# Attention and scan on one core: sums and products of the side work taken later, softmax sums inverted on chip

## The chip, the cores and the metric

The kernel runs on one core of one Trainium2 chip. The metric is device time in microseconds (us). Three timed runs of the kernel before gave 12563.84, 12565.47 and 12583.97 us; the median is 12565.47 us. Its profiled execution took 12592.85 us.

## The reference

Sixteen images of 256 channels by 1024 positions go through two layers, each added to its input after a group norm of 16 groups.

Layer 0 is attention with four heads of 32 and a small feed-forward part:

```
tok = group_norm(x) + pos
q, k, v = layer_norm(tok) @ w_qkv
out = softmax(q k' / sqrt(32)) v
tok = out @ w_out + b_out + tok
tok = gelu(layer_norm(tok) @ w_ff1 + b_ff1) @ w_ff2 + b_ff2 + tok
x = x + tok
```

Layer 1 is a selective scan of 512 channels with 64 states over the 1024 positions. With delta, B, C and u computed from the group-normed x (projection, causal convolution of four taps, silu, softplus):

```
h[t] = exp(delta[t] * A) * h[t-1] + delta[t] * u[t] * B[t]      (512 x 64 states)
y[t] = sum over states of h[t] * C[t]
x = x + ((y + u * D) * silu(z)) @ w_o * sigmoid(conv(x))
```

All is float32 at the interface.

## The kernel before

**The scan sets the beat.** For each image the 512 x 64 states are cut into 256 units of 128 rows by 1024 positions; 16 images make 4096 units. One unit takes, in the order in which the loop records it: a load of `dub` (delta times u, repeated over the states) six units ahead on SP's queue; `inputs`, a GpSimd multiply of `dub` with `bt` four units ahead (L977); a part of `outputs`, in which TensorE multiplies finished states `h` with C into `yb` (L1019, L1031) and ScalarE copies `y` and `yo` out; `scan` on VectorE (L994); and `decay` two units ahead, two TensorE products (L986) and one exponential on ScalarE (L988) into the PSUM tile `a`. There are two buffers of `a`, so the products for unit n+2 wait until scan n has read its own.

**Side work.** Everything else of the next image (`prepare`: `first_norm`, `attention_layer`, `scan_inputs`) and the end of the image before (`gate_and_store`) is written as generators. Each `yield w` ends a step; `w` is its share. After `scan` and `decay` of a unit the loop takes the next steps that are due:

```
return share if share < 1 else max(1.0, share / rate)
```

`rate` is chosen so that all shares of an image fill 247 units. A step's instructions thus stand on each engine's queue behind that unit's scan (VectorE), decay products (TensorE) and exponential (ScalarE). At the end of the kernel each of PE, ACT, DVE and POOL is bound to the order in which instructions were recorded. The first image's `prepare` runs alone, before any scan; I call that the prologue. The preparation of the other 15 images runs beside the scan of the image before.

**Places that the change touches.** In `group_norm` TensorE sums squares or values over channels into `gn_m_ps` or `gn_v_ps` (L275), `mean_of` reduces that on VectorE (L282), ScalarE makes the mean (L293) or the inverse root (L309, L310), and VectorE subtracts (L297) or multiplies (L313). It runs twice per image. In `attention_layer` the keys come out of TensorE as `qk_ps` (L431), ScalarE copies them to `k4` (L435), VectorE takes the difference `kd` of the two halves (L448), and the row maxima follow (L473, L481, L453). Then for two pairs of heads and two halves of the queries eight steps each make scores `st_ps` (L547), their exponentials `pt` (L555) and the products with the values, `av` (L535); the last product of a half is followed in the same step by `evacuate`, which copies 32 rows of the output to `ao` (L523) and 32 rows of the softmax sums to `sums` (L524), and the second head of the pair follows a step later. The sums go to DRAM (`den`), come back as a 128 x 32 tile `few`, are inverted (L579), go to DRAM again and come back repeated over 32 rows each; VectorE multiplies `ao` with them (L591). `o_ps` (L600) and `f_ps` (L618, L635) are the output and feed-forward products, added to the tokens at L596, L605 and L631. L615 adds the tokens to x. In `scan_inputs` `project` (L706, L711, L712) makes u, and `tap` (L720) is its convolution.

PSUM: beside the scan the side work has two banks of the pool `mm` through `psum`, and with `psum3` also the bank that holds `av`.

Of the kernel before, what the change touches and what calls it, by code (L numbers as in the profile page):

```python
# [19 lines left out]
P = 128  # L20
# [30 lines left out]
def attention_then_scan_kernel(  # L51
# [63 lines left out]
    def psum(name, dims=P):  # L115
        return (bank(mm, name) if beside["scan"] else free_bank(name))[:dims]
# [7 lines left out]
    def work(name, n=L):  # L124
        return wide.tile([P, L + 2 + CONV], F32, name=name, tag="wide")[:, :n]
# [4 lines left out]
    def hs(h):  # L130
        return ts(h, HL)
# [140 lines left out]
    def group_norm(src, dst):  # L272
        def sum_of(part, sums, k):
            for h in range(2):
                nc.tensor.matmul(  # L275
                    sums, share, part[:, hs(h)],
                    start=(k == 0 and h == 0), stop=(k == KC - 1 and h == 1),
                )

        def mean_of(sums):  # L280
            m = small.tile([P, NG], F32, name="gn_s", tag="gn_s")
            nc.vector.tensor_reduce(  # L282
                m, sums.rearrange("p (h g t) -> p g h t", g=NG, t=2), AX.XY, ALU.add
            )
            return m

        s = psum("gn_m_ps")
        sum_of(src[0], s, 0)
        yield 1
        sum_of(src[1], s, 1)  # L290
        yield 1
        m = s[:, :NG]
        nc.scalar.copy(m, mean_of(s))  # L293
        yield 1
        qs = []
        for k in range(KC):
            nc.vector.tensor_tensor(grouped(dst[k]), grouped(src[k]), over_group(m), ALU.subtract)  # L297
            q = work("gn_sq")
            nc.scalar.activation(q, dst[k], AF.Square)
            qs.append(q)  # L300
            yield 1
        s = psum("gn_v_ps")
        sum_of(qs[0], s, 0)
        yield 1
        sum_of(qs[1], s, 1)
        del qs, q
        yield 1
        v = s[:, :NG]
# [56 lines left out]
    def fetches(to, src, n=KC):  # L365
        return [partial(fetch, to, src, k) for k in range(n)]
# [18 lines left out]
    def attention_layer(b):  # L385
# [41 lines left out]
        for i in range(2):  # L427
            for hf in range(2):
                ps = psum("qk_ps")
                for k in range(KC):  # L430
                    nc.tensor.matmul(  # L431
                        ps, wqk_s[:, k, ts(i, P)], xn[k][:, hs(hf)], start=(k == 0), stop=(k == KC - 1)
                    )
                if i == 1:
                    nc.scalar.copy(k4[:, hs(hf)], ps)  # L435
                else:
                    for e in range(2):
                        nc.scalar.activation(
                            qm[hf][:, :, ts(e, 64)], ps.rearrange("p (c q) -> p c q", q=64),
                            AF.Identity, scale=even[:, e : e + 1],  # L440
                        )
                yield 1.5
# [2 lines left out]

        mx = small.tile([P, 2 * 2 * NJ], F32, name="mx", tag="mx")
        kd = hwork("kd")
        nc.vector.tensor_tensor(kd, k4[:, hs(0)], k4[:, hs(1)], ALU.subtract)  # L448
        waiting = []

        def maxima():
# [69 lines left out]
        def evacuate(pair, hf, e):  # L521
            h, o = 2 * pair + e, 2 * DH * e
            nc.scalar.copy(ao[ts(h, DH), hs(hf)], av[o : o + DH])  # L523
            nc.scalar.copy(sums[ts(h, DH), hs(hf)], av[o + DH : o + 2 * DH])  # L524

        for pair in range(HEADS // 2):
            qa, ka = qas[pair], kas[pair]
# [36 lines left out]
            yield 1  # L564


        den = dram.tile([2, HEADS, L], F32, name="den", tag="den")
        nc.sync.dma_start(den[0], sums[::DH, :])
        few = small.tile([P, HEADS * L // P], F32, name="few", tag="few")
        rows = [den[i].rearrange("h (p c) -> (h p) c", c=HEADS * L // P) for i in range(2)]  # L570
        yield 1
        nc.sync.dma_start(few, rows[0])
        yield 1
        tok = []
        for go in fetches(tok, kept):
            go()
            yield 0.5
        yield 0.5
        nc.vector.reciprocal(few, few)  # L579
        yield 1  # L580
        nc.sync.dma_start(rows[1], few)
        yield 1
        for h in range(HEADS):
            nc.sync.dma_start(sums[ts(h, DH)], den[1, h : h + 1].partition_broadcast(DH))
            if h % 2 == 1:
                yield 0.5
        yield 0.5
        yield 0.5
        outs = []
        for hf in range(2):  # L590
            nc.vector.tensor_tensor(ao[:, hs(hf)], ao[:, hs(hf)], sums[:, hs(hf)], ALU.mult)  # L591
            for k in range(KC):
                for i, ps in outs:
                    if i == k:
                        t = tok[k][:, hs(0)]
                        nc.vector.scalar_tensor_tensor(t, ps, col("b_out", k), t, ALU.add, ALU.add)  # L596
            outs.clear()
            for k in range(KC):
                ps = psum("o_ps")
                nc.tensor.matmul(ps, wout_s[:, 0, ts(k, P)], ao[:, hs(hf)], start=True, stop=True)  # L600
                outs.append((k, ps))
            yield 1.3
        for k, ps in outs:
            t = tok[k][:, hs(1)]
            nc.vector.scalar_tensor_tensor(t, ps, col("b_out", k), t, ALU.add, ALU.add)  # L605
        del outs, ps
        yield 1.2

        xs = []
        xn = [work("xn2") for _ in range(KC)]  # L610
# [1 line left out]
        hdn = work("hdn")  # L612
        f1 = []
        for hf in range(2):
            nc.vector.tensor_tensor(xs[hf], xs[hf], tok[hf], ALU.add)  # L615
            ps = psum("f1_ps")
            for k in range(KC):
                nc.tensor.matmul(  # L618
                    ps, wff1_s[:, k, :], xn[k][:, hs(hf)], start=(k == 0), stop=(k == KC - 1)
                )  # L620
            f1.append(ps)
            yield 1.1
# [1 line left out]
            table("gelu")  # L624
            nc.scalar.activation(hdn[:, hs(hf)], f1[hf], AF.Gelu, bias=col("b_ff1"))
        yield 2
        outs = []
        for hf in range(3):
            for k, ps in enumerate(outs):
                t = xs[k][:, hs(hf - 1)]  # L630
                nc.vector.scalar_tensor_tensor(t, ps, col("b_ff2", k), t, ALU.add, ALU.add)  # L631
            outs = []
            for k in range(KC if hf < 2 else 0):
                ps = psum("f2_ps")
                nc.tensor.matmul(ps, wff2_s[:, 0, ts(k, P)], hdn[:, hs(hf)], start=True, stop=True)  # L635
                outs.append(ps)
            yield 1.2
        state[b]["xs"] = xs
        state[b]["xr"] = dram.tile([C, L], F32, name="xr", tag="xr")

    def scan_inputs(b):
# [104 lines left out]
        project(0, 0)  # L746
        yield 1
        project(0, 1)
        yield 1
        for d in range(ND):  # L750
            for t in range(2):
                tap(d, t)
# [438 lines left out]
```

## Time and profile before

| | |
|---|---|
| timed runs, median | 12565.47 us |
| profiled execution | 12592.85 us, span 12590.8 us, granted TensorE clock 0.820 |
| DVE busy | 11064.3 us (88%) |
| POOL busy | 10050.9 us (80%) |
| PE busy | 9574.8 us (76%) |
| ACT busy | 7506.0 us (60%) |
| DMA share of the hardware queue | 65.3% |
| one scan (L994), mean | 2273 ns, 4096 of them |
| one `dub` multiply (L977), mean | 2404 ns, 4096 of them |
| first `few` inversion, in the prologue | at 234.51 us |

In the answers of the trace a line reads: start, length, engine, source line, operation, out<-in, shape, count, and in brackets how long the engine was idle before and what ended that. In the list of waits the numbers are total us, how often, and the longest. In the table of stretches each engine has its busy time and, in brackets, its number of instructions, then the granted TensorE clock, the share of DMA time and GB/s. TensorE's float32 products appear as two records each, so `x4` is two instructions.

### The profile page before, as it was taken

The page shows a single profiled execution, that of the slowest core. Times are in us where ns is not written, and L with a number is a line of the kernel's source. Part 1 is how long each engine was busy: PE and PEld are TensorE (multiplying, and loading weights), DVE is VectorE, ACT ScalarE, POOL GpSimd, SP SyncE. Part 2 cuts the span into 40 slices and gives each one's busy share as a digit, 9 for nine tenths or more (in the row PEclk, how much of TensorE's full clock was granted, in tenths as well). Part 3 has the DMA queues.
Part 4 walks back from the last instruction along what each step waited for, and adds up shares of the span by engine and source line. Part 5 has one row for each costly group of instructions (what it writes and reads, how often), then busy time and mean ns, then how long its engine had stood idle before and what let it go on. Part 6 is the DMA issues. An engine that isn't in the chain of part 4 may idle for free.

```text
span 12590.8 us, 419601 instructions
## 1 busy us (share of the span) xinstructions
PE 9574.8 (76%) x183984; PEld 5140.4 (41%) x183984; DVE 11064.3 (88%) x7355; ACT 7506.0 (60%) x10792; POOL 10050.9 (80%) x4233
## 2 busy tenths in 40 slices
PE   6686877868778687886868778687786877868777
PEld 2343434434344343443434344343443434434344
DVE  2788998989989899898989989899898998989998
ACT  3565665656656565665656656566565655656554
POOL 0587878878788787887878878787887878878798
PEclk8887988879788797987879888797887978879756
DMA  1566666676766766666676666766666666676666
GB/s 53 189 229 238 224 221 234 228 243 215 232 235 226 240 225 228 232 226 234 227 238 219 225 233 225 243 218 226 231 227 236 219 225 236 224 239 225 229 238 225
DMA packets 1070400, 2819.80 MB, mean 224 GB/s; under 512 B 324433, under 2 KB 402513, under 8 KB 1068562
## 3 DMA queue, kind: packets, MB, share of 16 engines
q1 hardware_dynamic: 1068562, 2792.97, 65.3%
q8 instruction: 1437, 23.54, 0.8%
q14 instruction: 401, 3.28, 0.1%
HBM read 2513.82 MB, written 261.62 MB: 220 GB/s over the span
## 4 chain that ended last, share of the span: by engine, by line
DVE 37%; PE 31%; issue 13%; ACT 8%; DMA 7%; POOL 3%; SPq 1%; DVEq 0%; POOLq 0%; ACTq 0%
DVE h L994 28%; PE a L986 5%; PE yb L1019 5%; ACT a L988 4%; DMA dub<-dus 3%; POOL dub L977 3%; PE av L535 2%; DVE over L453 2%; PE st_ps L547 2%; PE m_ps L908 2%; PE z_ps L684 2%; PE s_ps L473 2%; DMA xs<-ud 2%; DVE u L720 1%; PE gn_v_ps L275 1%
## 5 line engine op out<-in xcount | busy, mean ns | idle before, releaser
L977 POOL TENSOR_TENSOR dub<-dub,bt 128x1024 f32<-128x1024 f32 x4096 | 9752.7, 2404 | 2130.0 <-DMA dub<-dus 1928.2
L994 DVE TENSOR_TENSOR_SCAN h<-a,dub 128x1024 f32<-128x1024 f32 x4096 | 9166.7, 2273 | 596.0 <-ACT a L988 314.3
L988 ACT ACTIVATE a<-a,acol 128x1024 f32<-128x1024 f32 x4096 | 4466.1, 1090 | 3125.6 <-PE a L986 3065.8
L986 PE MATMUL a<-pieces,pick 48*128 48x512 bf16 x8192 | 1875.8, 448 | 2444.5 <-DVE h L994 2333.4
L1019 PEld LDWEIGHTS yb<-h,cd 128*32 128x32 f32 x131072 | 2433.3, 126 | 2822.9 <-issue 1601.6
L1019 PE MATMUL yb<-h,cd 128*32 128x64 f32 x131072 | 3189.4, 248 | 341.0 <-ACT y L1025 203.3
L986 PEld LDWEIGHTS <-pick 48*128 48x128 bf16 x8192 | 594.4, 95 | 2852.7 <-issue 2194.0
L1025 ACT COPY y<-yb 128x256 f32<-128x256 f32 x2048 | 766.5, 374 | 699.1 <-PE yb L1019 691.4
L1031 PE MATMUL yb<-turn,y 128*32 128x16 f32 x32768 | 590.7, 214 | 5.3 <-issue 4.4
L555 ACT ACTIVATE pt<-st_ps 128x512 f32<-128x512 f32 x1024 | 554.3, 599 | 63.8 <-PE st_ps L547 62.6
L535 PE MATMUL av<-pt,vv 128*64 128x512 f32 x2048 | 588.9, 655 | 3.8 <-ACT sums L524 1.6
L547 PE MATMUL st_ps<-sp 33*128 33x512 f32 x2048 | 573.6, 626 | 3.3 <-ACT pt L555 3.3
L1031 PEld LDWEIGHTS yb<-turn,y 128*32 128x32 f32 x32768 | 572.4, 159 | 6.0 <-issue 4.5
L1035 ACT COPY yo<-yb 128x128 f32<-128x128 f32 x512 | 136.4, 266 | 488.9 <-PE yb L1031 472.3
L734 PE MATMUL g_ps<-xp,w 128*128 128x512 f32 x732 | 406.9, 668 | 0.0
L473 PE MATMUL s_ps<-kd,qm 64*128 64x512 f32 x1022 | 340.6, 612 | 21.2 <-DVE kd L448 14.6
L453 DVE CUSTOM_DVE_ANT_0 over<-s_ps,over 128x512 f32<-128x512 f32 x512 | 325.9, 671 | 24.7 <-PE s_ps L473 24.4
L720 DVE SCALAR_TENSOR_TENSOR u<-up,cwh,u 128x1024 f32<-128x1024 f32 x192 | 295.8, 1541 | 28.0 <-ACT u L712 27.7
L481 ACT ACTIVATE over<-s_ps 128x512 f32<-128x512 f32 x511 | 275.2, 594 | 41.4 <-PE s_ps L473 41.4
L908 PE MATMUL m_ps<-xs,w 128*128 128x512 f32 x504 | 279.2, 704 | 10.2 <-POOL xs L887 9.4
L706 PE MATMUL u_ps<-xp,w 128*128 128x512 f32 x512 | 280.0, 674 | 1.5 <-ACT u L712 1.4
L661 POOL TENSOR_TENSOR xp<-xp,xs 128x1024 f32<-128x1024 f32 x32 | 75.1, 2349 | 254.1 <-DVE xp L313 246.5
(183 smaller groups left out, 7316.7 us busy)
## 6 DMA issues: line engine op xcount, KB each, us to landing
dub<-dus SPq DMA_DIRECT2D x4096, 512.0 KB
dps<-pc SPq DMA_DIRECT2D x384, 128.0 KB
pieces<-dps SPq DMA_DIRECT2D x1024, 48.0 KB
xs<-in_x_dram SPq DMA_DIRECT2D x64, 512.0 KB
xs<-kept SPq DMA_DIRECT2D x64, 512.0 KB
zs<-z SPq DMA_DIRECT2D x64, 512.0 KB
ud<-u SPq DMA_DIRECT2D x64, 512.0 KB
dus<-du SPq DMA_DIRECT2D x64, 512.0 KB
```

The source lines that it names most:

```text
L453: nc.vector.tensor_tensor_reduce(r, s, r, 1.0, -3.0e38, ALU.add, ALU.max, mx[:, at : at + 1])
L473: nc.tensor.matmul(s, qm[c // NJ][r, c % NJ], keys[r], start=True, stop=True)
L535: nc.tensor.matmul(av[ts(e, 2 * DH)], vv[j // (NJ // 2)][:, j % (NJ // 2), 2 * pair + e, :], pts[e], start=(j == 0), stop=(j == NJ - 1),)
L547: nc.tensor.matmul(s, ka[r, ts(j, P)], qa[r, hs(hf)], start=True, stop=True)
L555: nc.scalar.activation(pt, s, AF.Exp)
L977: nc.gpsimd.tensor_tensor(v, v, blocks[units[n][0]]["bt"], ALU.mult)
L986: nc.tensor.matmul(a[:, hs(hf)], w, pieces[r], start=True, stop=True)
L988: nc.scalar.activation(a, a, AF.Exp, scale=acol[:, at : at + 1])
L994: nc.vector.tensor_tensor_scan(now["h", e][:, i, :], decays.pop(n), loaded.pop(n), 0.0, ALU.mult, ALU.add)
L1019: nc.tensor.matmul(yb[ts(g, 32), ts(s, 64)], cd[:, at // 16, ts(c, 32)], hbuf[:, :, at : at + 8], start=(c == 0), stop=(c == 1),)
L1025: nc.scalar.copy(y2[:, r], yb[:, :256])
L1031: nc.tensor.matmul(some[ts(r, 32), x], y2[:, r, x:256:8], turn[:, x], start=True, stop=True)
```

## The change

- `group_norm`: the step after the last sum product has share 2 instead of 1, for the mean and for the variance.
- `kd` is taken from `k4`'s first half and the second half's PSUM tile; a step of share 1 follows it.
- `evacuate` copies the sums on VectorE instead of ScalarE.
- The four DMAs through `den` (seven issues per image) go. Eight TensorE products with columns of the identity turn the sums into a 128 x 32 PSUM tile `few_ps`; VectorE inverts it; ScalarE repeats it over 32 columns per head (`wide_few`, 128 x 1024); eight products with the identity turn that back into two PSUM tiles `inv_ps`, which VectorE multiplies into `ao`.
- Output and feed-forward products go through `outputs_of`: two products, then one at a time, each added a step after it was made; their PSUM tiles use the third bank too.
- The addition of the tokens to x (before L615) moves from VectorE to GpSimd.
- In `scan_inputs` the step behind `project(0, 1)` has share 2 instead of 1.

The sum of an image's shares goes from 272.3 to 279.2 (254.9 to 261.8 without the gate of an earlier image), so `rate` goes from 1.183 to 1.235 and steps with shares above 1.2 come a little closer together.

```diff
@@ group_norm
         sum_of(src[1], s, 1)
-        yield 1
+        yield 2
         m = s[:, :NG]
 ...
         sum_of(qs[1], s, 1)
         del qs, q
-        yield 1
+        yield 2
@@ attention_layer
                     nc.scalar.copy(k4[:, hs(hf)], ps)
+                    keys = ps
 ...
-        nc.vector.tensor_tensor(kd, k4[:, hs(0)], k4[:, hs(1)], ALU.subtract)
+        nc.vector.tensor_tensor(kd, k4[:, hs(0)], keys, ALU.subtract)
+        yield 1
 ...
             nc.scalar.copy(ao[ts(h, DH), hs(hf)], av[o : o + DH])
-            nc.scalar.copy(sums[ts(h, DH), hs(hf)], av[o + DH : o + 2 * DH])
+            nc.vector.tensor_copy(sums[ts(h, DH), hs(hf)], av[o + DH : o + 2 * DH])
 ...
-        nc.sync.dma_start(den[0], sums[::DH, :])
 ...
-        nc.sync.dma_start(few, rows[0])
 ...
-        nc.vector.reciprocal(few, few)
-        yield 1
-        nc.sync.dma_start(rows[1], few)
-        yield 1
-        for h in range(HEADS):
-            nc.sync.dma_start(sums[ts(h, DH)], den[1, h : h + 1].partition_broadcast(DH))
 ...
+        for j in range(NJ):
+            nc.tensor.matmul(ps[:, j], sums[:, ts(j, P)], ident[:, ::DH], start=True, stop=True)
+        fetch(tok, kept, 0)
+        yield 2
+        nc.vector.reciprocal(few, ps)
 ...
+        nc.scalar.copy(wide_few, few.unsqueeze(3).to_broadcast([P, NJ, HEADS, DH]))
 ...
+        yield 2
+        inv = []
+        for hf in range(2):
+            ps = psum3("inv_ps")
+            for j in range(NJ // 2):
+                w = wide_few[:, hf * (NJ // 2) + j]
+                nc.tensor.matmul(ps[:, ts(j, P)], w, ident, start=True, stop=True)
+            inv.append(ps)
+            yield 1
+
+        def times(hf):
+            nc.vector.tensor_tensor(ao[:, hs(hf)], ao[:, hs(hf)], inv[hf], ALU.mult)
+
+        def output(w, x, hf, k):
+            ps = psum3("o_ps")
+            nc.tensor.matmul(ps, w[:, 0, ts(k, P)], x[:, hs(hf)], start=True, stop=True)
+            return ps
+
+        def add_to(to, ps, bias, hf, k):
+            t = to[k][:, hs(hf)]
+            nc.vector.scalar_tensor_tensor(t, ps, col(bias, k), t, ALU.add, ALU.add)
+
+        def outputs_of(w, x, to, bias, ahead=None):
+            a, c = output(w, x, 0, 0), output(w, x, 0, 1)
+            if ahead:
+                ahead()
+            yield 1.4
+            add_to(to, a, bias, 0, 0)
+            add_to(to, c, bias, 0, 1)
+            a = output(w, x, 1, 0)
+            yield 1
+            add_to(to, a, bias, 1, 0)
+            c = output(w, x, 1, 1)
+            yield 1
+            add_to(to, c, bias, 1, 1)
+            yield 1
+
+        times(0)
+        yield 1
+        yield from outputs_of(wout_s, ao, tok, "b_out", partial(times, 1))
 ...
-            nc.vector.tensor_tensor(xs[hf], xs[hf], tok[hf], ALU.add)
-            ps = psum("f1_ps")
+            nc.gpsimd.tensor_tensor(xs[hf], xs[hf], tok[hf], ALU.add)
+            ps = psum3("f1_ps")
 ...
+        yield from outputs_of(wff2_s, hdn, xs, "b_ff2")
@@ scan_inputs
         project(0, 1)
-        yield 1
+        yield 2
```

More of the change, by code (lines that the diff above doesn't have):

```diff
@@ L564, in attention_layer @@
             yield 1
[L567 to L570, printed above, removed]
-        yield 1
-        nc.sync.dma_start(few, rows[0])
-        yield 1
[L574 to L579, printed above, removed]
@@ L580, in attention_layer @@
-        yield 1
-        nc.sync.dma_start(rows[1], few)
-        yield 1
-        for h in range(HEADS):
-            nc.sync.dma_start(sums[ts(h, DH)], den[1, h : h + 1].partition_broadcast(DH))
[L585 to L607, printed above, removed]
+        tok = []
+        few = small.tile([P, NJ, HEADS], F32, name="few", tag="few")
+        ps = psum("few_ps")[:, : NJ * HEADS].rearrange("p (j h) -> p j h", h=HEADS)
+        for j in range(NJ):
+            nc.tensor.matmul(ps[:, j], sums[:, ts(j, P)], ident[:, ::DH], start=True, stop=True)
+        fetch(tok, kept, 0)
@@ new lines, in attention_layer @@
+        yield 2
+        nc.vector.reciprocal(few, ps)
+        wide_few = work("wide_few").rearrange("p (j h d) -> p j h d", j=NJ, h=HEADS)
+        nc.scalar.copy(wide_few, few.unsqueeze(3).to_broadcast([P, NJ, HEADS, DH]))
+        wide_few = wide_few.rearrange("p j h d -> p j (h d)")
+        fetch(tok, kept, 1)
+        yield 2
[7 more added lines that the diff above has]
+            yield 1
@@ L609, in attention_layer @@
+        times(0)
+        yield 1
+        yield from outputs_of(wout_s, ao, tok, "b_out", partial(times, 1))
+        del inv, ps, wide_few
         xs = []
@@ L626, in attention_layer @@
         yield 2
[L627 to L637, printed above, removed]
+        del f1, ps
+        yield from outputs_of(wff2_s, hdn, xs, "b_ff2")
         state[b]["xs"] = xs
@@ L748, in scan_inputs @@
         project(0, 1)
-        yield 1
+        yield 2
         for d in range(ND):
```

## The prediction

> **What bounds the kernel now.** I read the page first, then VectorE's list of waits, then the table of stretches, then the timeline of single units. The page:
>
> ```profile
> PE 9574.8 (76%) x183984; PEld 5140.4 (41%) x183984; DVE 11064.3 (88%) x7355; ACT 7506.0 (60%) x10792; POOL 10050.9 (80%) x4233
> DVE 37%; PE 31%; issue 13%; ACT 8%; DMA 7%; POOL 3%; SPq 1%; DVEq 0%; POOLq 0%; ACTq 0%
> ```
>
> VectorE is the busiest, but TensorE carries almost as much of the chain that ended last. An image takes about 768 us in the middle of the kernel (from one image's first scan to the next one's): VectorE works 691 us (11064.3 / 16) and idles some 77. VectorE's list of waits:
>
> ```profile
> DVE h L994 <- ACT a L988: 314.3, 359, 7.5
> DVE few L579 <- DMA few<-den: 121.8, 12, 111.9
> DVE gn_s L282 <- PE gn_v_ps L275: 97.2, 31, 5.4
> DVE gn_s L282 <- PE gn_m_ps L275: 93.7, 33, 6.5
> DVE kd L448 <- ACT k L435: 32.5, 15, 10.0
> DVE u L720 <- ACT u L712: 27.7, 16, 5.0
> DVE ao L591 <- DMA sums<-den: 25.2, 16, 5.8
> ```
>
> The change aims at all but the first. The norms' sums look like the prize: beside the scan (the same list without the prologue has 91.8 and 79.4) they are 171.2 / 15 = 11.4 us an image. Whether they can be had is told by the sixth image's first norm:
>
> ```profile
> 4230.21 6.43 PE L275 MATMUL gn_m_ps<-xs,share 128*128 128x512 f32 x8
> 4237.16 0.39 PE L986 MATMUL a<-pieces,pick 48*128 48x512 bf16 x2
> 4236.68 0.69 DVE L282 TENSOR_REDUCE gn_s<-gn_m_ps 128x16 f32<-128x512 f32 x1 [4.75 <-PE gn_m_ps L275]
> 4237.59 1.09 ACT L988 ACTIVATE a<-a,acol 128x1024 f32<-128x1024 f32 x1 [6.18 <-PE a L986]
> 4240.59 2.28 DVE L994 TENSOR_TENSOR_SCAN h<-a,dub 128x1024 f32<-128x1024 f32 x1
> ```
>
> VectorE idles 4.75 us for the sum. But the decay products of a coming unit stand behind the same norm products on TensorE, and their exponential ends only at 4238.68. The loop scan, decay products, exponential, scan two units later (0.4 to 0.6, then 1.1, against two scans of 2.2) has little slack: what TensorE does in a unit is paid by VectorE as one wait or the other. So I cost every moved step by this chain.
>
> The attention stage (eight steps four times over) of the same image is TensorE's:
>
> ```profile
> 4479.20:4609.90 130.70, 119.68 (x2516) 58.69 (x2514) 118.41 (x53) 105.65 (x163) 121.49 (x53) 0.99 0.69 239
> ```
>
> PE is busy 119.68 of 130.70 us at clock 0.99, in 53 units, and VectorE idles about 13 us there (waits for exponentials 7.4, `yb` 2.7, `dub` 2.2, decay products 1.0).
>
> **The change, part by part, per image; plus is a gain.** Where steps fall I take from the order of the built changed kernel's instructions on each engine.
>
> *Norm sums, +1.8.* Three of four sums move one unit back; the second norm's mean stays in the unit after its products, for a share of 2 becomes 2 / 1.235 = 1.62 units. In the case above the third scan would run first, the sum would wait until 4236.68 as now, and the fourth scan would start with its exponential at 4238.75, not at 4240.59: 1.84 earlier, less the subtraction of 1.20 that now lies behind it: 0.6. The other two come out at 0.5 (there ScalarE's `cd` copies hold the exponential) and 0.7. Bounds: 0, and 10 if the whole waits went.
>
> *kd, +1.2.* It waits for `qk_ps` (TensorE ends at 4375.94) and not for ScalarE's copy, and runs 0.67 (L674, one operand in PSUM) instead of 1.16. The next scan starts at 4376.6, not 4377.82. Nothing is late next: maxima follow at VectorE's own pace.
>
> *tap, +1.5.* 22.7 / 15 beside the scan; ScalarE's u is ready a unit earlier. Bounds 0 and 2.8 (the wait plus the long first tap beside it).
>
> *Sums through TensorE, +0.7.* Gone are waits of 1.3 (`ao`) and 0.7 (`few`) and, with an operand in PSUM, 2 x (1.18 - 0.69) = 1.0. The DMA issues were hidden: SP's queue and the loads have six units of lead. Added: eight products of at most 86.1 / 256 = 0.34 each (L509) in one unit, 2.7 us of TensorE, which with `yb` (0.65) is 1.1 over the chain's slack of about 2.25; four and four later, 0.4 over; and the first `o_ps` pair, 2.0 to 3.8, is added one unit after it was made, a wait of 0 to 1.2, say 0.7. `wide_few` (1.05, as L299) fits into ScalarE's idle time. 3.0 - 2.2, rounded down; bounds -3 and +3. On `o_ps` the row is 3.78 for the first pair after an idle stretch and 1.98 for the second. The Trainium skill (TensorE: Matmul & The Clock Gate, Part 1) says that TensorE runs at half clock until it was busy for one window of about 3.4 us. By that rule the first pair is either wholly slow or wholly fast, and the wait would be 1.2 or 0 instead of 0.7, an estimate.
>
> *Feed-forward, -0.6.* Two additions of 1.53 (L615) leave VectorE. But the first `f_ps` pair takes 3.8 us of TensorE, and the additions now lie beside that chain; it would show as a wait for the exponential of the same size. The later products come one unit closer behind the gelu (one unit after it instead of two), and the chain over the table loads holds the scan as now (2.69 us at 4685.56). From the timeline, eight units would take 26.8 instead of 26.2 us. GpSimd gets 2 x 2.35 (L661); its lead of four units covers that; without the cover 4.7. Bounds -2 and +3.1. Against moving work to GpSimd stands the Trainium skill (Perfetto Trace Analysis, Optimizing Scalar/DVE Operations): the two engines share a port, so it might not help. By that rule VectorE instructions with two SBUF operands beside the additions would wait; there are none in those units, and the sum stays.
>
> *Sum copies on VectorE, -5.2.* This adds a wait. The copy for the first head stands right behind the value products of its own unit:
>
> ```profile
> 4512.39 0.39 PE L986 MATMUL a<-pieces,pick 48*128 48x512 bf16 x2 [0.37 <-DVE h L994]
> 4512.71 1.08 PE L535 MATMUL av<-pt,vv 128*64 128x512 f32 x4
> 4513.83 0.58 ACT L523 COPY ao<-av 32x512 f32<-32x512 f32 x1
> 4514.43 0.58 ACT L524 COPY sums<-av 32x512 f32<-32x512 f32 x1
> ```
>
> The unit's scan ends just before the decay products start at 4512.39; VectorE would wait until 4513.83, copy for 0.67 (no such row; L674 as the nearest on VectorE, ScalarE needs 0.58), and only then run the next scan: 1.44 + 0.67 and a handover of 0.1, 2.2 us, and 2.7 to 3.4 in the other three, where the products end later. Queued behind the copy are that scan and through it the next decay products, so TensorE idles about 2.0 us where it idled 0.4: 1.6 each, 6.4 for four. The four second copies wait for nothing and lie in VectorE's idle time. ScalarE loses eight copies (4.6 us), of which 0.3 per half was on the path: back 1.2. Bounds: -11.5 (four times 2.2 plus 2.7, nothing covered), 0 (all of it in the 13 us idle).
>
> *Closer steps, -2.0.* The attention steps take two units less, and those two plain units lie elsewhere at 2.19 instead of TensorE's 1.2 (0.39 + 0.65 + 0.14).
>
> Sum: 1.8 + 1.2 + 1.5 + 0.7 - 0.6 - 5.2 - 2.0 = -2.6; for 15 images 39 us longer.
>
> **The prologue** has no scan, and there the path is plain:
>
> ```profile
> 230.31 0.58 ACT L524 COPY sums<-av 32x512 f32<-32x512 f32 x1
> 230.91 0.58 SPq L568 DMA_DIRECT2D den<-sums  x1
> 234.51 0.35 DVE L579 RECIPROCAL few<-few 128x32 f32<-128x32 f32 x1 [111.92 <-DMA few<-den]
> 240.69 1.29 DVE L591 TENSOR_TENSOR ao<-ao,sums 128x512 f32<-128x512 f32 x2 [5.83 <-DMA sums<-den]
> ```
>
> 10.5 us from the last copy to the first output product at 241.43 become 2.7 + 0.35 + 1.05 + 2.7 + 0.4 for handovers = 7.2: 3.3. Two copies fewer on ScalarE after each of four halves: 4 x 1.15 = 4.6. kd about 1. Gain 9.
>
> So 39 - 9 = 30 us longer. The profiled execution (12592.85) would become 12623; it lies 27 us above the median of the runs shown, so the median goes to 12565.47 + 30 = 12595.
>
> **Rivals.** *Faster: the waits really go.* The attention stage's 13 us of VectorE idling take in the copies but for 1.5, and three sums bring 6 of their 10. Then 6 + 1.2 + 1.5 + 0.7 - 0.6 - 1.5 - 2.0 = +5.3 an image; 80 + 9 = 89 us less: 12477. For it: DVE is busiest, and ScalarE is relieved where it is 81% busy. Against: PE at 119.68 of 130.70. *Slower by more: the copies are not covered.* 11.5 less 1.2 gives -10.3 instead of -5.2; -7.7 an image, 107 us more: 12672. It decides wherever TensorE stands idle for the whole copy and scan. *No change:* copies at -3.2 instead of -5.2, the rest as summed: 9 us lost and 9 gained, 12565.
>
> **How the numbers follow.** Forecast 0.30 (alone 12590 to 12640), more slowly 0.16, no change 0.17, faster 0.37: my terms of both signs are of one size, so the faster case weighs heavily. About 0.2% (25 us) is what a measurement can tell. The range 12455 to 12680 takes in both rivals and leaves a tenth at each end.
>
> **What would show it.** Right: in the profile after, `gn_s` waits much shorter, but more `h <- ACT a`; four `sums <- PE av` waits an image of 1.5 to 2.7 us; the attention stage longer per unit with PE less busy; the first inversion in the prologue near 228 (234.51, less 3.5 for copies, 1 for kd, and the way through DRAM), not 234.51. Wrong: the waits `h <- ACT a` stay at 314 while those of the sums are gone, or `sums <- PE av` under 1 us.

## The result: 3.5% slower, and the profile after

The changed kernel takes 13007.28 us (median of 4 runs, 12985.68 to 13026.59) against 12571.45 us for the kernel before in the same comparison: a ratio of 1.0345, with a 95% interval of 1.0326 to 1.0365. The prediction was 12595 us with a range up to 12680; the change lost 436 us where 30 were foretold, and the sign alone was right. The profiled execution took 12985.68 us.

The page's line of engine totals and the group of the moved copies (busy us and mean ns of one, then the idle time before them and what ended most of it):

```profile
PE 9703.4 (75%) x184496; PEld 5263.5 (41%) x184496; DVE 11063.1 (85%) x7451; ACT 7510.7 (58%) x10680; POOL 10166.9 (78%) x4265
L526 DVE COPY sums<-av 32x512 f32<-32x512 f32 x128 | 88.2, 689 | 401.8 <-ACT ao L525 376.9
```

VectorE works as long as before (11063.1 against 11064.3 us) and the span is 393 us longer: it idles. The copies last 88.2 us, yet VectorE stood still for 401.8 us ahead of them, 376.9 of it for ScalarE's copy of `ao`. VectorE's list of waits says the same, and how the waits at which the change aimed came out:

```profile
DVE h L999 <- ACT a L993: 520.0, 462, 3.9
DVE sums L526 <- ACT ao L525: 376.9, 127, 27.7
DVE gn_s L282 <- PE gn_m_ps L275: 55.6, 32, 9.2
DVE kd L449 <- ACT k L435: 37.3, 15, 11.2
DVE u L725 <- ACT u L717: 6.5, 2, 5.0
DVE gn_s L282 <- PE gn_v_ps L275: 5.5, 1, 5.5
```

The norms' sums went from 190.9 to 61.1 us, the tap's wait from 27.7 to 6.5, and both waits for transfers of the softmax sums are gone. The wait of `kd` for ScalarE is not. `h <- ACT a` is 206 us longer too, but section 1 shows that most of this does not come with the copies. Without the prologue (the same list from the first scan on) it is

```profile
DVE sums L526 <- ACT ao L525: 312.4, 120, 4.2
```

120 waits are eight for each of 15 images, 2.6 us each. Where they stand is told by the table of stretches. The attention stage of the same image as in the prediction (four times eight steps) took 130.70 us before, and after:

```profile
4622.39:4782.29 159.90, 128.67 (x2519) 61.21 (x2517) 122.19 (x61) 105.12 (x160) 124.79 (x54) 0.88 0.56 189
```

TensorE has the same work in it (2519 instructions against 2516) but is busy 128.67 of 159.90 us instead of 119.68 of 130.70, and its granted clock in the stage is 0.88 where it was 0.99. The timeline of the end of one half of the queries shows both heads' copies:

```profile
4654.20 1.08 PE L537 MATMUL av<-pt,vv 128*64 128x512 f32 x4
4655.36 0.58 ACT L525 COPY ao<-av 32x512 f32<-32x512 f32 x1
4655.97 0.68 DVE L526 COPY sums<-av 32x512 f32<-32x512 f32 x1 [2.17 <-ACT ao L525]
4656.68 2.29 DVE L999 TENSOR_TENSOR_SCAN h<-a,dub 128x1024 f32<-128x1024 f32 x1
4659.03 0.39 PE L991 MATMUL a<-pieces,pick 48*128 48x512 bf16 x2 [3.16 <-DVE h L999]
4660.47 1.08 ACT L557 ACTIVATE pt<-st_ps 128x512 f32<-128x512 f32 x2
4661.57 0.58 ACT L525 COPY ao<-av 32x512 f32<-32x512 f32 x1
4662.19 0.69 DVE L526 COPY sums<-av 32x512 f32<-32x512 f32 x1 [3.22 <-ACT ao L525]
4662.91 2.29 DVE L999 TENSOR_TENSOR_SCAN h<-a,dub 128x1024 f32<-128x1024 f32 x1
```

VectorE's copy of the first head starts when ScalarE's copy of the same tile `av` has ended, 2.17 us after VectorE came free. It holds the scan, the scan holds the decay products (TensorE idles 3.16 us), those hold the next scores and their exponentials `pt`, and behind `pt` stands ScalarE's second copy, for which VectorE's second one waits 3.22 us. All eight copies of an image wait like this, not four.

Per image in the middle of the kernel (my own sum over the scans' starts) the time went from 768.5 to 795.8 us. In the attention stage the time beyond an undisturbed scan per unit (2.19 us) went from 17.0 to 46.6 us; all other stages together gained a little over 2 us.

### The profile page after: what moved, and what is told of

It is laid out like the page before. It is cut to its first block, busy times and chain, and to the rows that moved or that the text cites. A ratio compares the mean times of both kernels' runs of the same rounds, so it can differ in the third digit from the quotient of the medians.

```text
span 12983.7 us, 420360 instructions
## 1 busy us (share of the span) xinstructions
PE 9703.4 (75%) x184496; PEld 5263.5 (41%) x184496; DVE 11063.1 (85%) x7451; ACT 7510.7 (58%) x10680; POOL 10166.9 (78%) x4265
## 4 chain that ended last, share of the span: by engine, by line
PE 36%; DVE 36%; issue 12%; ACT 8%; DMA 5%; POOL 3%; SPq 1%; DVEq 0%; POOLq 0%; ACTq 0%
DVE h L999 26%; PE yb L1024 6%; PE a L991 6%; ACT a L993 4%; PE st_ps L549 3%; PE av L537 3%; DMA dub<-dus 3%; POOL dub L982 2%; DVE over L455 2%; PE z_ps L689 2%; PE s_ps L475 2%; PE m_ps L913 2%; PE yb L1036 2%; DMA xs<-ud 1%; DVE u L725 1%
## 5 line engine op out<-in xcount | busy, mean ns | idle before, releaser
L549 PE MATMUL st_ps<-sp 33*128 33x512 f32 x2048 | 607.1, 670 | 3.5 <-ACT pt L557 3.5
L526 DVE COPY sums<-av 32x512 f32<-32x512 f32 x128 | 88.2, 689 | 401.8 <-ACT ao L525 376.9
L689 PE MATMUL z_ps<-xp,w 128*128 128x512 f32 x508 | 277.7, 673 | 2.1 <-ACT z_t L695 1.4
L475 PE MATMUL s_ps<-k,qm 64*128 64x512 f32 x1024 | 267.4, 596 | 5.7 <-ACT over L483 5.4
```

The source lines that it names most:

```text
L475: nc.tensor.matmul(s, qm[c // NJ][r, c % NJ], keys[r], start=True, stop=True)
L549: nc.tensor.matmul(s, ka[r, ts(j, P)], qa[r, hs(hf)], start=True, stop=True)
```

## Experiments

Each is compared with the kernel before on the same chip. That kernel's medians lay between 12567.93 and 12585.55 us, single runs between 12524.58 and 12616.15. "The kept version" below is the changed kernel with the copies of the sums back on ScalarE.

### 1. The copies alone, and without them

In the first, one line of the changed kernel is undone; in the second, that line is the only change to the kernel before (line numbers there are those of the kernel before).

```diff
# sums_back: from the changed kernel
-            nc.vector.tensor_copy(sums[ts(h, DH), hs(hf)], av[o + DH : o + 2 * DH])
+            nc.scalar.copy(sums[ts(h, DH), hs(hf)], av[o + DH : o + 2 * DH])
# sums_alone: from the kernel before
-            nc.scalar.copy(sums[ts(h, DH), hs(hf)], av[o + DH : o + 2 * DH])
+            nc.vector.tensor_copy(sums[ts(h, DH), hs(hf)], av[o + DH : o + 2 * DH])
```

> The changed kernel with one line undone: the softmax sums are copied on ScalarE again. Theory A (the copies on VectorE are the whole loss, because each waits for ScalarE's copy of the same PSUM tile): the attention stage loses its 27 us an image and what is left of the change is my other terms, +2.6 - 2.0 + 2.0 an image and some 4 us in the prologue, so 12500 to 12560 us, at or below the kernel before. Rival B (the way of the sums through TensorE and the denser steps carry a good part of the loss): above 12750 us.

> The kernel before with that one line changed: sums copied on VectorE, nothing else. A: the whole loss comes with it, some 27 us in each of 15 images less 4 us in the prologue, 12940 to 13020 us; VectorE waits about 370 us in 128 copies for ScalarE's copy. B: at most half of that, below 12800 us.

Measured: 12532.01 us without them, ratio 0.9961 (0.9946 to 0.9976), a little faster than the kernel before; 13012.65 us with them alone, ratio 1.0343 (1.0328 to 1.0359), as slow as the whole change. The one line carries the whole loss. VectorE's waits for the exponential, in the kept version and then with the copies alone:

```profile
DVE h L999 <- ACT a L993: 448.6, 459, 3.6
```

```profile
DVE h L994 <- ACT a L988: 317.2, 332, 7.7
```

The kernel before has 314.3. So of the 206 us more in the changed kernel 134 come without the copies, where the norms' sums wait some 130 us less; the copies add 71 on top of the rest of the change, and only 3 on the kernel before. In the kept version the attention stage of the sixth image is as before:

```profile
4477.87:4608.13 130.26, 120.85 (x2486) 58.81 (x2487) 116.07 (x53) 104.65 (x162) 120.86 (x53) 0.97 0.67 226
```

Because all that follows is measured against the kept version, it was run again in more rounds, on another chip.

> The changed kernel with the sums copied on ScalarE once more, in more rounds. If the gain is real, the ratio to the kernel before lies within 0.994 to 0.998 again, some 25 to 55 us less. Rival (the four runs were lucky, as the versions next to it suggest): 0.999 to 1.002.

12543.42 us against 12585.55: ratio 0.9963 (0.9949 to 0.9976). The gain of some 43 us is real, and this version beats both kernels. Below, "against the kept version" means a kernel's distance from the kernel before in its own comparison, plus 43 us. By the two intervals these 43 us can be 30 to 68, and a kernel's own distance is good to some 15 to 25 us, so small distances say nothing.

### 2. What the copies wait for

The first of these records VectorE's copy ahead of ScalarE's, in the same step. The second also records it a step later, so that it stands behind value products that ended long before.

```diff
# vector_first
+            nc.vector.tensor_copy(sums[ts(h, DH), hs(hf)], av[o + DH : o + 2 * DH])
             nc.scalar.copy(ao[ts(h, DH), hs(hf)], av[o : o + DH])
-            nc.vector.tensor_copy(sums[ts(h, DH), hs(hf)], av[o + DH : o + 2 * DH])
# sums_later: sums_of(pair, hf, e) is the same copy; evacuate() has only ScalarE's
                     if j == 0 and hf == 1:
+                        sums_of(pair, 0, 0)
+                        sums_of(pair, 0, 1)
                         evacuate(pair, 0, 1)
 ...
+            sums_of(pair, 1, 0)
+            sums_of(pair, 1, 1)
             evacuate(pair, 1, 1)
```

> The changed kernel with the two copies of evacuate recorded in the other order, VectorE's first; work and steps are the same. A: VectorE no longer waits for ScalarE, the second head's copy waits for nothing, and only the wait for TensorE that I had predicted is left (1.5 to 2.7 us, four an image): 12560 to 12680 us. Rival C (VectorE waits for the scores or for TensorE whatever the order): within 60 us of 13007 us.

> The changed kernel with the copies of the softmax sums still on VectorE, but recorded one step after the value products, and ahead of ScalarE's second copy; so they wait neither for TensorE nor for ScalarE. Theory A (the loss is the order of two readers of one PSUM tile, and VectorE standing before it): the waits of sums are gone, what is left is at most the copying itself, 128 x 0.69 = 88 us, part of it in VectorE's idle time: 12535 to 12625 us, against 12532 with the copies on ScalarE. Rival (work on VectorE in a stage that TensorE bounds costs its full chain wherever it stands): as with VectorE's copy recorded first, 12750 to 12800.

Measured: 12785.03 us (ratio 1.0164, 1.0147 to 1.0181) and 12668.43 us (ratio 1.0074, 1.0058 to 1.0090). Both lie above what theory A gave: the order of the two readers is the largest part, but not all. VectorE's list of waits from the first scan on, with VectorE's copy first and then with the copies a step later:

```profile
DVE sums L525 <- PE av L537: 99.7, 60, 3.1
```

```profile
DVE sums L525 <- ACT ao L529: 8.1, 16, 1.5
```

With VectorE first, only the first heads' copies wait (60, four an image), for their own value products, 1.7 us each. With the copies a step later the waits are all but gone (8.1 us in all), and still 138 us are lost. Against the kept version:

| copies on VectorE | us more | what it adds |
|---|---|---|
| a step later | 138 | the copying itself (88 us of VectorE); the rest is presumably what it holds up |
| same step, VectorE first | 252 | 114 more: waiting for the value products with the scan behind |
| as changed, ScalarE first | 479 | 227 more: waiting for ScalarE's copy |

### 3. First heads or second heads

```diff
-            nc.vector.tensor_copy(
+            (nc.vector.tensor_copy if e == 0 else nc.scalar.copy)(    # first_heads; e == 1 in second_heads
                 sums[ts(h, DH), hs(hf)], av[o + DH : o + 2 * DH]
             )
```

> The changed kernel with only the first heads' sums copied on VectorE, the second heads' on ScalarE. Theory A (each copy on VectorE waits for ScalarE's copy of the same tile, first and second heads alike): about half of the 475 us between this version with all copies on ScalarE (12532) and the changed kernel: 12680 to 12790. Rival (the prediction's: the second heads' copies cost nothing, so the first carry everything): about 13000.

> The changed kernel with only the second heads' sums copied on VectorE, the first heads' on ScalarE. Theory A: the second heads' copy stands behind ScalarE's exponentials of the scores and its own copy, and costs as much as the first or more: 12700 to 12840, with waits sums <- ACT ao of 2 to 3.5 us each. Rival (the prediction's: they wait for nothing): 12525 to 12550.

Measured: 12774.23 us (ratio 1.0164, 1.0148 to 1.0179) and 12839.76 us (ratio 1.0211, 1.0194 to 1.0228): 249 and 315 us against the kept version. The second heads' copies, which the prediction priced at nothing, cost more than the first heads'. Theory A holds. The sum, 564, is above 479, so the two losses overlap in the changed kernel; where they do is not shown, since the waits themselves nearly add up (141.3 and 186.0 alone, 312.4 together). VectorE's list of waits from the first scan on, with the second heads' copies on VectorE:

```profile
DVE sums L526 <- ACT ao L525: 186.0, 60, 4.1
```

That is 3.1 us each; the first heads' wait 141.3 / 60 = 2.4 us.

### 4. The other parts one by one, on the kernel before

```diff
# norms_alone: both steps in group_norm
-        yield 1
+        yield 2
# trip_alone, shortened: the transfers through den replaced by few_ps, wide_few and inv_ps as in the change; old output loop
-            nc.vector.tensor_tensor(ao[:, hs(hf)], ao[:, hs(hf)], sums[:, hs(hf)], ALU.mult)
+            nc.vector.tensor_tensor(ao[:, hs(hf)], ao[:, hs(hf)], inv[hf], ALU.mult)
-                ps = psum("o_ps")
+                ps = psum3("o_ps")
# norms_and_trip: both
```

> The kernel before with the two norm steps at share 2 and nothing else. My term was +1.8 an image less a part of the closer steps (1 of the 2 us): 0 to 30 us less than before, 12540 to 12570 us. Rival D (the waits go in full, 9 us an image): 12430 to 12460 us.

> The kernel before with one part of the change alone: the softmax sums turned and inverted on chip, the output products still two and two. The prediction's term: +0.7 an image and 3.3 us in the prologue, so about 14 us less than before: 12550 to 12570. Rival (it is nearly the whole gain of the version with the copies back on ScalarE, 44 us, or more): 12500 to 12535.

> The kernel before with the inversion on chip and the two norm steps of share 2. Theory R (the norm steps alone cost 150 us because closer steps leave the transfers of the sums fewer units; the norms themselves gain 1.7 us an image): with the transfers gone the norm steps gain, so 15 to 35 us less than the inversion alone, and no waits for the sums' transfers. Rival (the norm steps shift every later stage against the scan, whatever the transfers do): about 150 us more than the inversion alone, near 12700.

Measured: 12725.0 us (ratio 1.0114, 1.0094 to 1.0135), 12641.23 us (1.0051, 1.0034 to 1.0068) and 12635.13 us (1.0053, 1.0033 to 1.0073). The first two missed all that was expected: parts that were to gain 27 and 14 us cost 149 and 67. The third tells part of why the first is so bad: the norm steps cost 149 us on the kernel before and nothing (-6 us, within the scatter) once the transfers are gone, though they do not gain the 15 to 35 us of theory R either. In the kernel with the norm steps alone VectorE's list of waits has

```profile
DVE few L579 <- DMA few<-den: 152.6, 16, 111.7
DVE ao L591 <- DMA sums<-den: 58.6, 16, 5.6
```

(they are whole lists, the prologue's longest waits included) against 121.8 and 25.2 before. More shares in an image raise `rate`, so steps follow each other in fewer units, and the round trip through DRAM no longer fits between them. These waits are 64 us of the 149. Of the rest some 46 us (3.1 an image, by the scans' starts) are lost in the attention stage, which has no such transfer; in the third kernel, without the transfers, that stage is longer by 3.9 us an image. So the transfers are one reason; for the rest the shift of other stages, the rival of theory R, is not excluded. The norms themselves did what they should: the stage of the first norm lost 14.5 us beyond the scans' pace where it lost 16.0.

The inversion alone gained 3.0 us an image in its own stage, from the first inversion to the second layer norm (0.9 if the layer norm's first step is counted in), and lost about 7 in others: 3 in the feed-forward stage and, by where it is cut, 3 to 4.5 in that of the taps and the gate's products. The instructions that write `u` there took 419 us instead of 400, which is 1.3 us an image; the other losses are not explained.

### 5. One part undone in the kept version

```diff
# norms_back: both steps in group_norm
-        yield 2
+        yield 1
# tap_back: behind project(0, 1)
-        yield 2
+        yield 1
# ff_back, shortened: the feed-forward part as before
-            nc.gpsimd.tensor_tensor(xs[hf], xs[hf], tok[hf], ALU.add)
-            ps = psum3("f1_ps")
+            nc.vector.tensor_tensor(xs[hf], xs[hf], tok[hf], ALU.add)
+            ps = psum("f1_ps")
 ...
-        yield from outputs_of(wff2_s, hdn, xs, "b_ff2")
+        for hf in range(3):       # f2_ps two and two, yield 1.2, as before
# kd_back
-        nc.vector.tensor_tensor(kd, k4[:, hs(0)], keys, ALU.subtract)
-        yield 1
+        nc.vector.tensor_tensor(kd, k4[:, hs(0)], k4[:, hs(1)], ALU.subtract)
```

> The version with the sums copied on ScalarE, and the two norm steps back at share 1. Theory T (each part is worth its own term wherever the others stand): the norms' term of +1.8 an image is lost, 27 us more than 12532: 12550 to 12570, with the waits of gn_s back at about 190 us. Theory P (a part moves every later step against the scan, and that is worth up to 60 us of either sign beside its own term): outside 12545 to 12575, the waits of gn_s back all the same.

> The version with the sums copied on ScalarE, and the step behind the second projection back at share 1. Theory T: the tap's term of +1.5 an image is lost, 22 us more: 12545 to 12565, with about 22 us of waits of u for ScalarE. Theory P: outside that, through the busy time of the taps and the waits in the gate's stage.

> The version with the sums copied on ScalarE, and the feed-forward part as before: the addition on VectorE, the products two and two in steps of 1.2, two PSUM banks. Theory T: the term of -0.6 an image comes back, 9 us less: 12515 to 12530. Rival (the additions on VectorE cost their 49 us, and the products two and two their waits): 12550 to 12590.

> The version with the sums copied on ScalarE, and the keys' difference as before: both operands from SBUF, no step of its own. Theory A (the difference waits for ScalarE's copy in both forms, so only the length of the instruction and the step differ): the waits of kd stay at 30 to 40 us, and the time within 20 us of 12532. Rival (the change of kd carries the gain of this version, by its shorter operation and its own step): 12555 to 12590.

| undone | median us | ratio, 95% | against the kept version | its term, 15 images |
|---|---|---|---|---|
| norms | 12576.28 | 1.0008 (0.9994 to 1.0021) | 49 | 27 |
| tap | 12723.78 | 1.0117 (1.0098 to 1.0136) | 197 | 22 |
| feed-forward | 12663.23 | 1.0069 (1.0053 to 1.0085) | 136 | -9 |
| kd | 12688.70 | 1.0086 (1.0065 to 1.0107) | 162 | 18 |

Each one costs more than its term, three of them several times as much. Theory T's bounds hold for none of the four, and for the feed-forward part and `kd` the rivals' bounds are passed as well; of what was expected the waits of the norms' sums came back (185.8 us). Taking away a share changes `rate`, and with it the fraction of a unit at which each later step falls. This is seen at the two steps that make the values `vv` (2.2 shares apart), just ahead of the attention's eight-step rounds: they stand two units apart in the kernel before, in the changed and in the kept version, and one unit apart in all four of these. The table of stretches for the eight units behind them (sixth image), in the kept version and with the tap's step back:

```profile
4477.87:4496.84 18.97, 17.06 (x382) 9.96 (x384) 17.72 (x9) 14.43 (x22) 17.95 (x8) 1.00 0.72 252
```

```profile
4529.49:4553.94 24.45, 22.08 (x384) 11.48 (x384) 17.89 (x9) 14.82 (x23) 19.00 (x9) 0.79 0.51 175
```

TensorE's work is the same (382 and 384 instructions), but it takes 22.08 us instead of 17.06, at a granted clock of 0.79 instead of 1.00; the other three have 0.79 to 0.85 there. So in this image the shift costs 3.4 to 5.5 us at this one place. Over the attention stage these four lose 22.1 to 25.5 us beyond the scans' pace, against 18.2 in the kept version.

To tell the edit from the shift, two of them were undone again with the sum of the shares kept:

```diff
# tap_back_same_sum: the share of 2 stands behind the first projection
         project(0, 0)
-        yield 1
+        yield 2
         project(0, 1)
-        yield 2
+        yield 1
# kd_back_same_sum: SBUF operands as before, its own step kept
-        nc.vector.tensor_tensor(kd, k4[:, hs(0)], keys, ALU.subtract)
+        nc.vector.tensor_tensor(kd, k4[:, hs(0)], k4[:, hs(1)], ALU.subtract)
         yield 1
```

> The version with the sums copied on ScalarE, and the share of 2 behind the first projection instead of the second, so the tap is as close to its input as before but the sum of the shares is unchanged. Theory P (the 192 us of the run with the tap's step back at 1 came from steps falling on other units, the two value steps among them, one unit apart instead of two): they stand as in the first version, and only the tap's term of about 22 us is lost: 12540 to 12580. Rival (the distance of the tap itself is worth 192 us): near 12720.

> The version with the sums copied on ScalarE, the keys' difference with both operands from SBUF as before, but its own step kept, so the sum of the shares is unchanged. Theory P: the 157 us of the run without the step came from the step, and the form of the instruction is worth its 17 us of VectorE time at most: 12530 to 12560. Rival (the PSUM operand itself is worth the 157 us): near 12690.

Measured: 12605.25 us (ratio 1.0029, 1.0014 to 1.0043) and 12570.64 us (1.0002, 0.9991 to 1.0014): 80 and 46 us against the kept version, where it had been 197 and 162. So 117 and 116 us of those (differences of two runs each, good to some 30 us) were the shift and not the edit; the two steps of the values are two units apart again, and the attention stage is back at 17.7 and 18.5 us beyond the scans' pace. What is left is above theory P's bounds too. For the tap, 26 us of it is the wait of `u` that came back, and 28 us that the instructions which write `u` are longer (16 us against the second profile of the kept version); for `kd`, 21 us is its longer instruction (32.2 against 11.0 us in all). The rest of both is not explained.

### 6. kd ahead of ScalarE's copy

```diff
# kd_first: from the kept version, in the loop over the keys
+                    if hf == 1:
+                        nc.vector.tensor_tensor(kd, k4[:, hs(0)], ps, ALU.subtract)
                     nc.scalar.copy(k4[:, hs(hf)], ps)
```

> The version with the sums copied on ScalarE, and the keys' difference recorded ahead of ScalarE's copy of the second half of the keys, both of which read the same PSUM tile. Theory A: kd no longer waits for ScalarE (36.1 us, 15 times, in that version) but for TensorE, and starts about 0.7 to 1.2 us earlier in each image: 10 to 20 us less, 12512 to 12522. Rival (the wait is TensorE's products in truth): no change, 12527 to 12537.

Measured: 12590.99 us, ratio 1.0010 (0.9997 to 1.0022), 60 us more than the kept version. VectorE's list of waits from the first scan on:

```profile
DVE kd L437 <- PE qk_ps L431: 65.1, 15, 4.8
```

Recorded ahead, `kd` waits for TensorE alone: the wait for ScalarE was the order of recording. But the edit put it into the step of the products themselves, a step earlier than in the change, and so it waits more than twice as long (in the changed kernel 26.1 us from the first scan on). The experiment shows whose wait it was; as a trial of the gain it was badly placed.

## Why the prediction was wrong

*The failing step: "Sum copies on VectorE, -5.2".* Measured per image in the middle of the kernel it is -30.6 (765.2 in the kept version, 795.8 in the changed one), outside its bounds of -11.5 to 0. Three things in it failed; their sizes are from sections 2 and 3, and the second overlaps with the other two. First, "VectorE would wait until 4513.83": that is where ScalarE's copy of `ao` starts; I took the end of the value products for the releaser. Both copies read one PSUM tile, and the one recorded second waits until the first has ended: 227 us. Second, "the four second copies wait for nothing and lie in VectorE's idle time": they wait for ScalarE's second copy, which stands behind the exponentials of the scores, and those behind the decay products that the first stall had held up; alone they cost 315 us. Third, the value products' end with a scan behind the copy: this was the mechanism that I priced, at 1.6 us each because the rest was to be covered; its waits are 1.7 us each, within what I gave for them, but it and the copying itself cost 114 + 138 = 252 us, 16.8 an image over 15 images. So even without the order of readers the term was too small by a factor of three: in this stage VectorE's idle time is not spare. Copies that wait for next to nothing still cost 138 us, which fits that the chain scan, decay products, exponential, scan runs through VectorE. The bound of -11.5 was also too near by its own figures: it takes 2.2 us for each of the four first copies, where the same paragraph has 2.7 to 3.4 for three of them, which makes -13.0 to -15.1.

No line that I had read of the trace before shows two engines reading one PSUM tile, except where the second needs the first one's result (`z` and `z_t`, both from `z_ps`). But a page that I had not weighed bears on it. The Trainium skill (PSUM — Partial Sum Buffer, PSUM bank collisions raise a hardware error) says that two engines must not access the same bank in the same 32 partitions at once, reads included, and that software has to keep them apart, by bank and quadrant or simply by bank. The two copies read different sets of 32 partitions of the bank, so by the finer rule they would not have had to wait; the trace shows that here they did. No run shows them side by side: that was not tried.

*"kd, +1.2"*, which was to wait for `qk_ps` and not for ScalarE's copy, fell for a like reason: its wait is 37.3 us after and 32.5 before, and it is set by what was recorded ahead of it (section 6). Whether through `qk_ps`, which ScalarE reads too, or through the tile `k4`, whose other half that copy writes, the runs do not tell. Where its step falls counts too: with the tap's step back the same instruction waits 11.2 us in all. What it gained is its length: 11.0 us in all against 18.5 before.

*The rest came out as a sum.* Without the copies my terms make +2.6 an image and +4.4 in the prologue, 15 x 2.6 + 4.4 = 43 us; the kept version is 44 and 42 us faster. By stages, beyond the scans' pace:

| term | predicted | stage, before to kept version |
|---|---|---|
| norm sums | +1.8 | +1.4 in the first norm, -0.3 in the second |
| sums through TensorE | +0.7 | +2.0 from the first inversion on |
| tap | +1.5 | +2.8 up to the end of the taps |
| feed-forward | -0.6 | -1.1 |
| closer steps | -2.0 | -1.2 in the attention, -0.8 in the convolution |

That the sum fits this well is partly luck: sections 4 and 5 show that a single term holds only with the others in place, since a part that changes the shares moves all later steps, and in the two cases where the move was told from the edit it was worth some 116 us. The prediction had this only as "closer steps". The table is from one profile of each kernel, and its figures depend on where a stage is cut: the +2.0 is +0.6 if the first step of the layer norm is counted in. By the second profile of the kept version an image takes 766.6 instead of 765.2 us, so that the gain is 1.9 us and not 3.3. A single term of about 1 us is not confirmed by it.

*The prologue* of the changed kernel was 12.1 us shorter (first scan at 401.6 instead of 413.7) where 9 were foretold:

```profile
224.68 0.36 DVE L576 RECIPROCAL few<-few_ps 128x32 f32<-128x32 f32 x1 [1.75 <-PE few_ps L573]
```

That is 3 us earlier than the forecast 228, but both figures owe much to luck. The kept version and the one with the tap's step back record the same prologue, in which shares play no part. Yet their stretches from the first exponential of the scores to the first inversion differ, in this order:

```profile
130.90:232.20 101.30, 93.93 (x268) 23.34 (x268) 0.00 (x0) 43.83 (x80) 0.00 (x0) 0.73 0.05 20
132.90:222.90 90.00, 82.12 (x270) 21.64 (x268) 0.00 (x0) 43.84 (x80) 0.00 (x0) 0.84 0.06 23
```

The granted clock was 0.73 in one execution and 0.84 in the other. The changed kernel's profile had 0.84 there and took 89.80 us, as long as the second with all copies on ScalarE; the kernel before had 0.72 and took 103.90 us, 2.6 us more than the first. So no run shows the 4.6 us that the prediction gave to the copies in the prologue: at an equal clock they are worth 0.2 us, and the way through TensorE some 2.6 where it gave 3.3.

*What would show it:* shorter `gn_s` waits, more `h <- ACT a`, and a longer attention stage with TensorE less busy came true, the first two without the copies as well; "four `sums <- PE av` waits an image" became eight waits for ScalarE. The rival "the copies are not covered" named the right place. That its bound of 12672 is near 12668, where the copies a step later came out, is chance: it priced copies that wait, and these hardly do.

## What to carry to other kernels

When a copy moves to another engine, look at who else reads the same PSUM tile: a second reader on another engine may wait for the first one's end and, through it, for all that stands ahead of it on that engine's queue. An idle stretch of an engine is cover only if nothing that the bounding chain needs stands behind the moved instruction. Where steps are placed by shares, try a change of work with the sum of the shares kept, or the shift of the other steps is measured with it. And before a gain is read from one profile, compare the granted clock of that stretch in both.

## What the runs showed of the hardware that I had not expected

A tap of the convolution (VectorE, all operands in SBUF) usually takes 1.25 us, but up to 3.2 us (3.4 in the kernel before) when it starts beside a GpSimd multiply. From the kept version's timeline:

```profile
4012.82 2.34 POOL L982 TENSOR_TENSOR dub<-dub,bt 128x1024 f32<-128x1024 f32 x1 [0.20 <-DMA dub<-dus]
4013.08 3.17 DVE L725 SCALAR_TENSOR_TENSOR u<-up,cwh,u 128x1024 f32<-128x1024 f32 x1
```

The multiply ends at 4015.16, and the tap ends 1.09 us after that. The same holds for all 174 taps of this profile that start while GpSimd is at work: each ends 1.08 to 1.19 us after that instruction, and most start near its end, so that they keep their 1.25 us. Where the steps happen to fall decides how often this occurs: the 192 taps took 256.7 us in the kept version (267.8 in its second profile), 295.8 in the kernel before, 310.6 with the norms alone and 301.0 with the inversion alone. The scan, with an operand in PSUM, keeps its 2.27 us beside GpSimd (in the kernel before 2.274 us for the 2529 scans almost wholly beside a GpSimd instruction, 2.272 for the 127 beside none). The Trainium skill (SBUF — State Buffer, SBUF: two separate sides) says that a VectorE operation with two SBUF inputs and a GpSimd operation that reads SBUF hold a shared pair of ports one after the other, for the whole instruction. The trace agrees.
